# Attention with a depthwise convolution: nine key blocks to a batch, and normalized x kept in DRAM

## The chip, the cores and the metric

The kernel runs on one core of one Trainium2 chip. A time is the device time of one execution in microseconds. Profiled executions carry a record of every instruction of the engines: PE (TensorE), DVE (VectorE), ACT (ScalarE), POOL (GpSimd), and SP (SyncE), which issues nearly all DMAs here.

## The reference

All data is float32. With `ln` a layer norm over the 384 channels of a token, for each of 4 images of 48 x 48 = 2304 tokens:

```
x        (4, 384, 48, 48)                      # 8 heads of 48 channels
local    = batchnorm(depthwise_conv7x7(x))     # 49 taps a channel
q, k, v  = ln(x) @ qkv_w.T + qkv_b
q        = q + ln(local)
out      = softmax(q @ k.T * 48**-0.5) @ v     # per head, 2304 x 2304
y        = x + out @ proj_w.T + proj_b
```

## The kernel before

Channels lie on the 128 partitions in three chunks, two heads side by side (rows 0-47 and 64-111), so that the eight heads make four pairs; the fourth is gathered from the tails of the chunks by DMA (`kt`, `qt`). The tokens of an image fall into six groups of 384 (eight image rows), 24 groups t in all, and into 18 key blocks of 128.

**A group's slots.** The queries of a group t meet all keys of their image, pair by pair, in batches of `BATCH` = 6 key blocks: 3 batches a pair, `NSLOT` = 12 slots a group. In a slot PE first makes the scores of its batch (`scores`, L669, into a ring of three PSUM buffers `r`), ACT turns each into `pt` by an exponential (L673), and then PE weighs the values with the batch of the slot before (`weigh`, L684, into `sums`). Nine `pt` buffers hold the one and a half batches between. Slots 0 to 2 also make the next group's queries (`query_step`, between scores and weighing), slots 5, 8 and 10 the previous group's output projection (`output_step`).

**The end of a pair.** When the last batch of a pair has been weighed, `pair_end` copies `sums` out on ACT, in the middle of the next `scores` (after block `BATCH // 2 - 1`), and sends the softmax denominators to DRAM (`den`). For the last pair of a group, six gathers `ao<-aot` follow. Then `divide` fetches all denominators (`rd`), takes reciprocals on DVE (L601), sends them out (`rden`) and spreads them over the partitions (`rb`); its place is just after the scores of slot 2 of the next group.

**The work beside.** DVE convolves the image for the next group (L242, 147 instructions). `convolve("slot", t, s, half)` emits a number of them twice in each slot; a small plan (`spare`, `share`) fixes how many. Two layer norms run in pieces between: that of the convolved group ("local"), and that of one group of the next image's x (in the groups g = 1 to 5 of the first three images, 15 in all; the sixth group of an image is done while the keys are made). Each piece of a norm goes over several engines: a sum over the chunks and a transpose on DVE, a DMA trip (`parts`, `four`), the centring on DVE (L392), the squares on ACT (L339), the same sum and trip again, a root on ACT (L402 to L404), and the scaling on DVE. For the x of the next image they are spread over slots 3 to 8.

**Order.** For PE, DVE and ACT the order of the program is the order of the engine: each works its instructions one after the other, and one that waits holds up all behind it. SP's order is made by the framework. All six normalized groups of x stay in SBUF (`xn0` to `xn5`). Between two images stands a stage of keys and values (`keys_values`), 216 PE instructions.

Before the first group, a first stage loads the weights, normalizes the first image, makes its keys and values, and convolves its first group (partly on PE, L261).

Of the kernel before, what the change touches and what calls it, by code (L numbers as in the profile page):

```python
# [23 lines left out]
BATCH = 6  # L24
NSLOT = 12
X_SLOTS = 4, 7
OUT_SLOTS = 5, 8, 10
# [15 lines left out]
def unshifted_pass(  # L43
# [56 lines left out]
    xn = {}  # L100

    def load_x(b, g):
        t = big.tile([P, CC, G], F32, tag=f"xn{g}", name=f"xn{b}_{g}")
        load_packed(t, x[b, :, g * G : (g + 1) * G])
        xn[b, g] = t
# [52 lines left out]
    for c in range(CC):  # L158
# [17 lines left out]
        work.tile([P, 2, C], F32, tag="pt", name="pt", bufs=9) for _ in range(PE_TAPS * CC // 6)  # L176
# [6 lines left out]
    load_x(0, 1)  # L183
    load_packed(staged[0], qkv_wT[:, 0:C])
    for g in range(2, NG):
        load_x(0, g)
# [80 lines left out]

    def spare(t, s, half):
        b, g = divmod(t, NG)
        other = 0.0  # L270
        if b + 1 < B and g:
            other += {(3, 1): 2.0, (4, 1): 2.1, (5, 1): 2.0, (8, 0): 2.5}.get((s, half), 0.0)
        if t:
            other += {(2, 0): 0.7, (4, 1): 1.4}.get((s, half), 0.0)
            other += 0.6 if half and s in OUT_SLOTS else 0.0
        if t + 1 < NT:
            first, second = norm_slots(t)
            other += {
                (first - 1, 1): 2.0,
                (first, 1): 2.1,  # L280
                (first + 1, 1): 2.0,
                (second + 1, 0): 4.4,
            }.get((s, half), 0.0)
        return max(0.0, 4.0 - other)

    def norm_slots(t):
        return (6, 9) if t else (8, 10)

    points, room = [], []
    for t in range(NT):  # L290
        if t % NG == 0 and t:
            points += [("kv", t, g, h) for g in range(NG) for h in range(2)]
            room += [4.0, 2.0, 4.0, 2.0, 4.0, 2.0, 4.0, 4.0, 2.0, 4.0, 4.0, 4.0]
        points += [("slot", t, s, h) for s in range(NSLOT) for h in range(2)]
        room += [spare(t, s, h) for s in range(NSLOT) for h in range(2)]
    share = {pt: [] for pt in points}
    at = 0
    for t in range(1, NT):
        due = points.index(("slot", t - 1, norm_slots(t - 1)[0], 0))
        total, n, done, sofar = sum(room[at:due]), CC * KS * KS, 0, 0.0  # L300
        for i in range(at, due):
            sofar += room[i]
            upto = round(n * sofar / total)
            share[points[i]] += [t] * (upto - done)
            done = upto
        at = due
# [9 lines left out]
    def chunk_sum(src):  # L316
        s = work.tile([P, G], F32, tag="sum", name="sum")
        nc.vector.tensor_add(s, src[:, 0, :], src[:, 1, :])  # L318
        nc.vector.tensor_add(s, s, src[:, 2, :])  # L319
        return s  # L320

    def spread_mean(s):

        m = bank()
        nc.tensor.matmul(m[:, :G], lhsT=mean_w, rhs=s, start=True, stop=True)  # L325
        return m

    def spread_sum(src):

        m = bank()  # L330
        project(m[:, :G], lambda c: mean_w, lambda c: src[:, c, :])
        return m

    def centre(src, m):
        nc.vector.tensor_sub(src, src, over_chunks(m[:, :G]))  # L335

    def squares(src):
        sq = work.tile([P, CC, G], F32, tag="sq", name="sq", bufs=1)
        nc.scalar.activation(sq, src, AF.Square)  # L339
        return sq  # L340

    def inverse_root(m):

        y = work.tile([P, G], F32, tag="y", name="y", bufs=1)
        u = work.tile([P, G], F32, tag="u", name="u", bufs=1)
        nc.scalar.activation(u, m[:, :G], AF.Ln, bias=eps)
        nc.scalar.activation(y, u, AF.Exp, scale=-0.5)
        nc.scalar.activation(u, y, AF.Square)
        return m, y, u
# [4 lines left out]
    few = G // 32  # L354

    def sum_out(src):

        s = chunk_sum(src)
        blocks = work.tile([P, G], F32, tag="u", name="blocks", bufs=1)
        part = work.tile([P, few], F32, tag="part", name="part")  # L360
        parts = dram.tile([32, 4, few], F32, tag="parts", name="parts")
        four = work.tile([P, 4 * few], F32, tag="four", name="four")
        nc.vector.transpose(blocks, s)
        nc.vector.tensor_reduce(
            part, blocks.rearrange("p (k i) -> p k i", i=32), AX.X, ALU.add
        )
        nc.sync.dma_start(out=parts.rearrange("i q k -> q i k"), in_=part)
        nc.sync.dma_start(
            out=four,
            in_=parts.rearrange("i q k -> i (q k)")  # L370
            .rearrange("(o i) f -> o i f", o=1)
            .to_broadcast([4, 32, 4 * few]),
        )
        return four

    def sum_in(four):
        s = work.tile([P, few], F32, tag="few", name="few")
        nc.vector.tensor_reduce(
            s, four.rearrange("p (q k) -> p k q", k=few), AX.X, ALU.add
        )  # L380
        return s

    def spread(s):
        y = work.tile([P, G], F32, tag="y", name="y", bufs=1)
        nc.vector.transpose(
            y, s.rearrange("p (k i) -> p k i", i=1).to_broadcast([P, few, 32])
        )
        return y

    def centre_by(src, four):  # L390
        y = spread(sum_in(four))
        nc.vector.scalar_tensor_tensor(src, over_chunks(y), -1.0 / C, src, ALU.mult, ALU.add)  # L392

    def variance(four):
        s = sum_in(four)
        nc.vector.tensor_scalar(s, s, 1.0 / C, LN_EPS, ALU.mult, ALU.add)
        return s

    def few_root(v):
        y = work.tile([P, few], F32, tag="few_y", name="few_y")  # L400
        u = work.tile([P, few], F32, tag="few_u", name="few_u")
        nc.scalar.activation(u, v, AF.Ln)  # L402
        nc.scalar.activation(y, u, AF.Exp, scale=-0.5)
        nc.scalar.activation(u, y, AF.Square)  # L404
        return v, y, u

    def few_newton(v, y, u):
        nc.vector.tensor_mul(u, u, v)
        nc.vector.scalar_tensor_tensor(u, u, -1.0, y, ALU.add, ALU.mult)
        nc.vector.scalar_tensor_tensor(y, u, -0.5, y, ALU.mult, ALU.add)  # L410
        return spread(y)

    def newton(m, y, u):
        nc.vector.scalar_tensor_tensor(u, m[:, :G], eps, u, ALU.add, ALU.mult)
        nc.vector.scalar_tensor_tensor(u, u, -1.0, y, ALU.add, ALU.mult)
        nc.vector.scalar_tensor_tensor(y, u, -0.5, y, ALU.mult, ALU.add)
        return y
# [129 lines left out]
    def query_end(t, rs):  # L547
# [3 lines left out]
        nc.vector.tensor_mul(acc, acc, over_chunks(rs))  # L551
# [105 lines left out]
    def scores(t, s):  # L657
# [4 lines left out]
        for kb in range(k0, k0 + BATCH):  # L662
# [9 lines left out]
            pt = work.tile([P, 2, G], F32, tag="pt", name="pt", bufs=9)  # L672
            nc.scalar.activation(pt, r[:, :, :G], AF.Exp, scale=SCALE)  # L673
            batch.append((kb, pt))
            if kb == k0 + BATCH // 2 - 1:
                pair_end()
        weighing.append((t, p, batch))
# [35 lines left out]
    src = xn[0, 0]  # L713
    m = spread_sum(src)
# [3 lines left out]
    centre(src, m)  # L718
    sq = squares(src)
# [3 lines left out]
    m = spread_sum(sq)  # L723
    root = inverse_root(m)
# [3 lines left out]
    nc.vector.tensor_mul(src, src, over_chunks(newton(*root)))  # L728
# [3 lines left out]
    for g in range(NG):  # L732

        last = g == NG - 1
        src = accs[0] if last else xn[0, g + 1]
        making = keys_values(0, g)
        next(making)
        convolve_first(8 if last else 4)
# [4 lines left out]
        s = chunk_sum(src)  # L743
# [4 lines left out]
        m = spread_mean(s)  # L748
        convolve_first(4)
        centre(src, m)  # L750
        sq = squares(src)
        if not last:
            next(making)
        convolve_first(3)
        m = spread_mean(chunk_sum(sq))
        root = inverse_root(m)
        next(making)
# [6 lines left out]
        if last:  # L764
            r, r2 = ring(), ring()
            for u, m in enumerate((r[:, 0], r[:, 1], r2[:, 0])):
                query_step(0, u, m)
        else:
            first_products(5 if g < 4 else 0)
        convolve_first(8)  # L770
        rs = newton(*root)
        if last:
            query_end(0, rs)
        else:
            nc.vector.tensor_mul(src, src, over_chunks(rs))

    for t in range(NT):
        b, g = divmod(t, NG)
        if g == 0 and b:
# [3 lines left out]
            src = xn[b, NG - 1]  # L783
            for gk in range(NG):
                making = keys_values(b, gk)
                next(making)
                if gk == 4:
                    rs = few_newton(*root)
                    nc.vector.tensor_mul(src, src, over_chunks(rs))
                convolve("kv", t, gk, 0)  # L790
                next(making)
                if gk == 3:
                    root = few_root(variance(four))
                convolve("kv", t, gk, 1)
                if gk == 0:
                    four = sum_out(src)
                if gk == 1:
                    centre_by(src, four)
                if gk == 2:
                    four = sum_out(sq)  # L800
                next(making)
                if gk == 1:
                    sq = squares(src)
        following = t + 1 < NT
        coming = None
        sent = {}
        first, second = norm_slots(t)
        for s in range(NSLOT):
            scores(t, s)

            if s == 2 and t:
                rb = divide(t - 1)
            if s == 0 and not following:

                ending = big.tile([P, CC, G], F32, tag="xn0", name="ending")
                nc.gpsimd.memset(ending[:, 0, :], 0.0)
                for j in range(2):
# [6 lines left out]
                    )  # L824
# [631 lines left out]
```

## Time and profile before

| | |
|---|---|
| median of 3 runs | 3011.69 us (3011.38 to 3012.81) |
| the profiled execution | 3014.8 us, span 3013.0 us, mean granted clock 0.998 |
| PE busy | 2979.3 us (99%), 15698 matmul instructions |
| DVE busy | 2300.9 us (76%) |
| ACT busy | 1560.7 us (52%) |
| DMA | 98.83 MB, 14.3% of the engines' time on the queue of SP |

A row of the instruction groups names the line, the engine, the operation, what it writes and reads, how many there are, their busy time and the mean duration, and how long the engine stood idle before them and for whom. Matmuls overlap in the pipeline, so the mean duration of one (490 ns) is longer than the time between two starts. Each matmul of the program is two instructions in the trace, and those of the two heads of a pair start together (6 to 7 ns apart).

### The profile page before, as it was taken

To read this page: it belongs to the slowest core of one execution; us is meant where nothing else is said; L and a number is where in the kernel's file an instruction comes from. 1 tells how busy PE (TensorE), PEld (TensorE's weight loads), DVE (VectorE), ACT (ScalarE), POOL (GpSimd) and SP (SyncE) were. 2 spreads that over 40 slices of the span, in tenths; PEclk is the share of its full clock that TensorE was granted. 3 is DMA by queue.
4 is the path that set the end of the run, shared out by engine and by line. 5 is a ranking of instruction groups with operands and counts; after the bars stand their busy time and mean duration, and the time that the engine had idled before them with its cause. 6 is when DMAs were issued, how large, how long until landed. Compare 5 with 4: busy or idle time off the path is not lost.

```text
span 3013.0 us, 42331 instructions
## 1 busy us (share of the span) xinstructions
PE 2979.3 (99%) x15698; PEld 1358.1 (45%) x15698; DVE 2300.9 (76%) x4556; ACT 1560.7 (52%) x2385; POOL 24.3 (1%) x71
## 2 busy tenths in 40 slices
PE   7999999999999999999999999999999999999998
PEld 4544444444454444444454444444445444444443
DVE  6899988887666899888755888987876488788411
ACT  4455555555435555555534555555552555555553
POOL 2000000000000000000000000000000000000000
PEclk9999999999999999999999999999999999999999
DMA  6111111011111111111110111012010111100001
GB/s 108 39 25 21 34 36 45 20 38 41 30 26 33 36 33 32 34 35 34 32 30 23 35 38 45 21 34 48 27 30 19 28 27 33 25 26 19 17 26 29
DMA packets 97868, 98.83 MB, mean 33 GB/s; under 512 B 42850, under 2 KB 88435, under 8 KB 97652
## 3 DMA queue, kind: packets, MB, share of 16 engines
q1 hardware_dynamic: 96192, 95.86, 14.3%
q8 instruction: 125, 2.05, 0.3%
q14 instruction: 91, 0.75, 0.1%
q0 software_dynamic: 960, 0.07, 0.0%
q10 hardware_dynamic: 500, 0.11, 0.0%
HBM read 70.19 MB, written 15.24 MB: 28 GB/s over the span
## 4 chain that ended last, share of the span: by engine, by line
PE 95%; DVE 3%; DMA 1%; ACT 0%; issue 0%; POOL 0%; SPq 0%; ACTq 0%; DVEq 0%; POOLq 0%
PE r L669 38%; PE o L684 37%; PE m L422 10%; PE r L422 9%; DVE acc L242 2%; PE o L261 0%; PE m L325 0%; DMA staged<-in_qkv_wT_dram 0%; DMA columns<-bias 0%; PE r L890 0%; DMA bias<-row 0%; DMA taps_in<-in_conv_w_dram 0%; DMA vec<-natural 0%; DVE xn L335 0%; DVE sum L319 0%
## 5 line engine op out<-in xcount | busy, mean ns | idle before, releaser
L673 ACT ACTIVATE pt<-r 128x768 f32<-128x768 f32 x1728 | 1276.3, 812 | 1166.1 <-PE o L684 740.3
L242 DVE SCALAR_TENSOR_TENSOR acc<-slab,vec,acc 128x368 f32<-128x368 f32 (+8 forms) x3429 | 1736.7, 583 | 6.5 <-DMA vec<-natural 3.3
L684 PE MATMUL o<-pt,v 128*49 128x384 f32 x6912 | 1173.8, 489 | 0.1
L669 PE MATMUL r<-q,k 48*128 48x384 f32 x5184 | 908.2, 496 | 0.0
L684 PEld LDWEIGHTS o<-pt,v 128*49 128x49 f32 x6912 | 425.8, 124 | 709.0 <-issue 682.1
L669 PEld LDWEIGHTS r<-q,k 48*128 48x128 f32 x5184 | 439.6, 185 | 467.3 <-ACT pt L673 226.4
L669 PE MATMUL r<-qt,kt 48*128 48x384 f32 x1728 | 300.2, 493 | 0.0
L647 DVE SCALAR_TENSOR_TENSOR xr<-m,pb,xr 128x384 f32<-128x384 f32 x69 | 42.5, 616 | 282.9 <-PE m L422 282.9
L669 PEld LDWEIGHTS r<-qt,kt 48*128 48x128 f32 x1728 | 150.5, 185 | 149.4 <-ACT pt L673 67.8
L422 PE MATMUL r<-xn,w_qk 128*128 128x384 f32 x450 | 152.3, 491 | 0.7 <-ACT q L545 0.7
L422 PE MATMUL m<-ao,w_o 128*128 128x384 f32 x414 | 152.0, 503 | 0.4 <-DVE ao L868 0.4
L422 PE MATMUL m<-xn,w_qk 128*128 128x384 f32 x414 | 152.0, 503 | 0.0
L422 PE MATMUL r<-w_v,xn 128*128 128x384 f32 x432 | 144.5, 487 | 4.2 <-DVE xn L728 2.4
L422 PEld LDWEIGHTS r<-xn,w_qk 128*128 128x128 f32 x450 | 86.7, 193 | 62.4 <-issue 3.0
L318 DVE TENSOR_TENSOR sum<-sq 128x384 f32<-128x384 f32 x47 | 26.1, 555 | 112.7 <-ACT sq L339 112.7
L422 PEld LDWEIGHTS r<-w_v,xn 128*128 128x128 f32 x432 | 81.7, 190 | 62.8 <-issue 4.7
L422 PEld LDWEIGHTS m<-ao,w_o 128*128 128x128 f32 x414 | 73.0, 189 | 74.6 <-issue 13.6
L422 PEld LDWEIGHTS m<-xn,w_qk 128*128 128x128 f32 x414 | 73.0, 189 | 74.2 <-issue 27.8
L462 ACT COPY v<-r 128x384 f32<-128x384 f32 x72 | 32.1, 481 | 134.8 <-PE r L422 134.8
L601 DVE RECIPROCAL rd<-rd 128x24 f32<-128x24 f32 (+2 forms) x25 | 7.5, 301 | 123.6 <-DMA rd<-den 123.6
L458 ACT ACTIVATE k<-r,qkb 128x384 f32<-128x384 f32 x72 | 39.3, 580 | 65.6 <-PE r L422 65.6
L584 ACT COPY ao<-o 49x384 f32<-49x384 f32 x141 | 66.7, 473 | 1.7
(118 smaller groups left out, 821.1 us busy)
## 6 DMA issues: line engine op xcount, KB each, us to landing
xr<-in_x_dram SPq DMA_DIRECT2D x24, 576.0 KB
out_dram<-xr SPq DMA_DIRECT2D x72, 192.0 KB
slab<-in_x_dram SPq DMA_DIRECT2D x32, 378.0 KB
xn<-in_x_dram SPq DMA_DIRECT2D x48, 216.0 KB
rb<-rden SPq DMA_DIRECT2D x48, 216.0 KB
slab<-in_x_dram SPq DMA_DIRECT2D x16, 297.0 KB
slab<-in_x_dram SPq DMA_DIRECT2D x32, 126.0 KB
xn<-in_x_dram SPq DMA_DIRECT2D x48, 72.0 KB
```

What stands on the lines that cost most here:

```text
L242: nc.vector.scalar_tensor_tensor(dst, src, weight, dst, ALU.mult, ALU.add)
L318: nc.vector.tensor_add(s, src[:, 0, :], src[:, 1, :])
L422: nc.tensor.matmul(dst, lhsT=weights(c), rhs=src(c), start=c == 0, stop=c == CC - 1)
L458: nc.scalar.activation(k[:, u, :], r[:, j, :G], AF.Identity, bias=qkb[:, 1, u : u + 1])
L462: nc.scalar.copy(v[:, u + NB, :, 0:HD], r[:, j, :C].rearrange("p (h d) -> p h d", d=HD))
L584: nc.scalar.copy(dst[r : r + HA], sums[r : r + HA, :G])
L601: nc.vector.reciprocal(rd, rd)
L647: nc.vector.scalar_tensor_tensor(xr[:, co, :], m, pb[:, co : co + 1], xr[:, co, :], ALU.add, ALU.add)
L669: nc.tensor.matmul(r[:, j, :G], lhsT=kk[:, blk * P : (blk + 1) * P], rhs=qq, start=True, stop=True)
L673: nc.scalar.activation(pt, r[:, :, :G], AF.Exp, scale=SCALE)
L684: nc.tensor.matmul(sums[r : r + HA, :G], lhsT=values[t // NG, kb // NB][:, kb % NB, 2 * p + j, :], rhs=pt[:, j, :], start=kb == 0, stop=kb ...
```

## The change

- `BATCH` 6 becomes 9 and `NSLOT` 12 becomes 8: two batches a pair. `pt` has 15 buffers in place of 9. `pair_end` is called in `scores` after block 5 of 9 (it was block 2 of 6).
- `xn0` to `xn5` go. A normalized group of x is written to DRAM (`keep_x`) and read back (`fetch_x`) for the keys and for the queries; SBUF holds one raw group (`xa`) and two normalized ones (`xn`).
- The buffers `sum`, `y` and `u` of the norms go; sums, means and roots live in parts of the one buffer `sq` (class `Norm`).
- The pieces of the norms, the output steps (slots 3, 4, 5), the call of `divide` (slot 1) and the plan of the convolution get new places. In the first stage the last part of the last group's keys stands before the second mean, and the convolution's counts there are 13, 4, 3, 7 (8, 4, 3, 8 before).

The core of the diff (the class `Norm` takes over the bodies of the old helpers):

```
-BATCH = 6
-NSLOT = 12
-X_SLOTS = 4, 7
-OUT_SLOTS = 5, 8, 10
+BATCH = 9
+NSLOT = 8
+QUERY_SLOTS = 0, 1, 2
+OUT_SLOTS = 3, 4, 5
...
+    def x_tile(tag):
+        return work.tile([P, CC, G], F32, tag=tag, name=tag, bufs=1 if tag == "xa" else 2)
...
+    def keep_x(b, g):
+        kept[b, g] = dram.tile([P, CC, G], F32, tag=f"kept{g}", name=f"kept{b}_{g}")
+        nc.sync.dma_start(out=kept[b, g], in_=xn[b, g])
+
+    def fetch_x(b, g):
+        xn[b, g] = x_tile("xn")
+        nc.sync.dma_start(out=xn[b, g], in_=kept[b, g])
...
+        time = 6.0
+        if half == 0:
+            time += 2.1 * (s in QUERY_SLOTS) * (t + 1 < NT) + 2.1 * (s in OUT_SLOTS) * (t > 0)
...
+            time -= {(0, 1): 2.2, (1, 1): 4.4, (2, 1): 2.9}.get((s, half), 0.0)
...
+            time -= {(1, 0): 0.7, (2, 0): 1.4}.get((s, half), 0.0)
...
-            pt = work.tile([P, 2, G], F32, tag="pt", name="pt", bufs=9)
+            pt = work.tile([P, 2, G], F32, tag="pt", name="pt", bufs=15)
...
-            if kb == k0 + BATCH // 2 - 1:
+            if kb == k0 + BATCH - 4:
                 pair_end()
+                if between:
+                    between()
...
-        convolve_first(8 if last else 4)
+        convolve_first(13 if last else 4)
...
-        if not last:
-            next(making)
+        next(making)
...
+                if gk < 4:
+                    fetch_x(b, gk + 2 if gk < 3 else 1)
...
+            scores(t, s, between)
+
+            if s == 1 and t:
                 rb = divide(t - 1)
...
+            if s == 2 and t:
+                ao = outputs[t - 1][0]
+                nc.vector.tensor_mul(ao, ao, rb)
+
+            if s == 4:
+                if coming:
+                    load_x(b + 1, g)
+                if g < NG - 1 and t + 2 < NT:
+                    fetch_x(*divmod(t + 2, NG))
+                elif coming and g == NG - 1:
+                    fetch_x(b + 1, 0)
+                    fetch_x(b + 1, 1)
             convolve("slot", t, s, 0)
...
             if weighing[0][0] != t or s:
                 weigh()
...
+            if coming and g:
+                if s == 1:
+                    norm_x.few_centre()
+                    norm_x.squares()
+                if s == 2:
+                    norm_x.few_variance()
+                    norm_x.few_root()
+            if t and following:
+                if s == 5:
+                    norm.few_centre()
+                    norm.squares()
+                if s == 6:
+                    norm.few_variance()
+                    norm.few_root()
             convolve("slot", t, s, 1)
...
+            if coming and g:
+                if s == 0:
+                    norm_x = Norm(xn[b + 1, g - 1])
+                    norm_x.sum()
+                    norm_x.out()
+                if s == 1:
+                    norm_x.sum_squares()
+                    norm_x.out()
+                if s == 2:
+                    norm_x.scale(norm_x.few_newton())
+                    keep_x(b + 1, g - 1)
```

## The prediction

> **What bounds the kernel now.** The page comes first: the span, the busy shares, and the chain that ended last, by engine.
>
> ```profile
> span 3013.0 us, 42331 instructions
> ...
> PE 2979.3 (99%) x15698; PEld 1358.1 (45%) x15698; DVE 2300.9 (76%) x4556; ACT 1560.7 (52%) x2385; POOL 24.3 (1%) x71
> ...
> PE 95%; DVE 3%; DMA 1%; ACT 0%; issue 0%; POOL 0%; SPq 0%; ACTq 0%; DVEq 0%; POOLq 0%
> ```
>
> PE sets the end. The change takes no matmul away, so it can gain only what PE loses between batches, and it loses whatever makes PE wait. Everything then hangs on the order within a slot, so the second view is the timeline, here slot 1 of a group with an x norm, all engines (start, duration, engine, line, what, count):
>
> ```profile
> 591.26 4.21 PE L669 MATMUL r<-q,k 48*128 48x384 f32 x24
> 592.28 2.21 ACT L673 ACTIVATE pt<-r 128x768 f32<-128x768 f32 x3 [1.39 <-PE r L669]
> 594.37 0.97 ACT L584 COPY aot<-o 49x384 f32<-49x384 f32 x2
> 594.87 0.73 SPq L585 DMA_DIRECT2D den<-aot  x2
> 595.40 2.20 PE L422 MATMUL m<-xn,w_qk 128*128 128x384 f32 x6
> 595.65 4.53 SPq L589 DMA_DIRECT2D ao<-aot  x6
> 597.53 4.08 PE L684 MATMUL o<-pt,v 128*49 128x384 f32 x24
> ...
> 600.28 0.53 SPq L598 DMA_DIRECT2D rd<-den  x1
> ...
> 602.14 0.30 DVE L601 RECIPROCAL rd<-rd 128x24 f32<-128x24 f32 x1 [6.62 <-DMA rd<-den]
> ```
>
> PE runs without a gap: scores 4.14 us, query step 2.13, weighing 4.01. The last pair of the previous group is copied out 3.11 us into the slot, and 7.77 us later the denominators are back, where DVE had waited 6.62 us. Over the groups in which DVE waited, copy to reciprocal was 6.8 to 7.9 us, mostly 6.9. Slot 2 had begun at 601.54, so they came back at about its start, which is where `divide` stands.
>
> **Part 1, the batches.** Inside a batch the pairs of matmuls start every 0.3225 us, a key block every 0.645. Twelve make 3.87; so a weighing batch pays 0.14 at its borders, and a scores batch 0.27, of which 0.06 is a wait for the ring (batches without it take 4.08). The ring matters more with nine blocks. Block i needs the exponential of block i - 3 to be over, and ACT is slower than PE, as the first scores of all show:
>
> ```profile
> 145.84 4.15 PE L669 MATMUL r<-q,k 48*128 48x384 f32 x24
> ...
> 146.81 4.32 ACT L673 ACTIVATE pt<-r 128x768 f32<-128x768 f32 x6 [0.28 <-PE r L669]
> ```
>
> Six take 4.32, one alone 0.81, so the step is (4.32 - 0.81) / 5 = 0.70. From block 5 on PE goes at ACT's step: 0.06, and 0.055 more for each of blocks 6 to 8, 0.23 in all. After: scores 18 x 0.3225 + 0.21 + 0.23 = 6.24, weighing 5.80 + 0.14 = 5.94, together 12.18. Before, one and a half slots: 12.21. So 192 slots gain 0.03 each, **-5.5 us**: the ring takes back nearly all that fewer borders give. Bounds: with no ring wait at all 12.18 - 0.23, thus -49; with the slowest three exponentials of the trace (2.35 for three, a step of 0.77), up to +0.07 x 4 blocks x 192 = +54. The step of 0.70 stands in nearly every run of three (2.21), so I keep -5.5.
>
> **Part 2, the x norm behind `divide`.** In the changed order, DVE's queue in slot 1 holds the reciprocal, 13 convolution instructions (14 in group 1; from the plan), the centring of x, 2 more, the sum of squares. ACT's holds six exponentials, the two copies, three exponentials, the query, *the squares of x*, and then the nine exponentials of slot 2. The squares need the centring, so the exponentials of slot 2 wait behind all of this. The pieces, as they are now:
>
> ```profile
> 621.83 0.24 DVE L378 TENSOR_REDUCE few<-four 128x12 f32<-128x48 f32 x1 [0.88 <-DMA four<-parts]
> 622.10 0.58 DVE L385 STREAM_TRANSPOSE y<-few 128x384 f32<-128x384 f32 x1
> 622.71 1.36 DVE L392 SCALAR_TENSOR_TENSOR xn<-y,xn 128x1152 f32<-128x1152 f32 x1
> ...
> 637.42 1.18 ACT L339 ACTIVATE sq<-xn 128x1152 f32<-128x1152 f32 x1
> ```
>
> Let the scores of slot 1 start at 0. The first exponential starts at 1.02 (592.28 - 591.26); the copies follow the sixth, 1.02 + 6 x 0.70 = 5.2 (now 1.02 + 3 x 0.70 = 3.1, as shown). The reciprocal comes 6.9 later, at 12.1. It and the two rows behind it take 0.65 (602.14 to 602.79); 13 convolutions at 0.50 (the row's 1736.7 / 3429 is 0.506, groups at an image's edge 0.47) take 6.5; the centring, 621.83 to 624.07, 2.24: 21.5. The squares end at 22.7.
>
> The scores of slot 2 start at 6.24 + 2.13 + 5.94 = 14.3, and the first exponential is wanted at 15.3. It is 7.4 us late. PE makes three blocks into the ring and stands. Nothing covers this: DVE can't come earlier, since it waits for `rd`, and coming later only makes it worse. Now the same squares stand behind the exponentials of a slot and the centring is long done (622.71 against 637.42).
>
> A stall has a second price. Two gaps of the first stage, first the rows in which PE waited, then the windows after them (columns: length, PE busy, granted clock, DMA share, GB/s):
>
> ```profile
> 31.51 4.11 PE L422 MATMUL r<-w_v,xn 128*128 128x384 f32 x12 [2.42 <-DVE xn L728]
> ...
> 132.72 1.60 PE L325 MATMUL m<-sum,mean_w 128*128 128x384 f32 x2 [4.16 <-DVE sum L319]
> ```
>
> ```profile
> 132.70:136.10 3.40, 3.38 (x6) 0.51 0.02 5
> ...
> 31.50:34.80 3.30, 3.29 (x10) 1.00 0.99 166
> ```
>
> After 2.4 us of idling PE goes on at full clock; after 4.2 us it has half the clock for 3.3 us, with pairs 0.64 apart. A stall of 7.4 lies beyond both. Then blocks 3 to 8 take 4.93 us from the first restart to the start of block 8 (five pairs at half speed, then full), where ACT's step alone would ask 5 x 0.70 = 3.50: 1.43 more. So 8.9 us a group, in 15 groups: **+133 us**. Bounds: without the clock's part 112; with copy to reciprocal 7.9 instead of 6.9, 148.
>
> The Trainium skill (TensorE: Matmul & The Clock Gate, Part 1) says that the clock halves after an idle window of about 3.4 us and comes back after as long a busy one, and that the window runs free of the program. It speaks against this change in the same way; by it alone a stall would cost up to 1.7 us more, an estimate, and the sum would end some 4 us higher.
>
> **Part 3, the rest of a group.** After the stall, DVE has some 13 us of idling at `rd` in a group (now 3 to 7), but its group holds 98 us of work (97.6 to 100.3 busy in 110.4 us in the windows by group) and now lasts 119. Followed on from 21.5: the variance of x is ready at 33, before slot 3 begins at 37.5, so its root on ACT holds nobody. In slot 5 the centring of the local norm ends about when the slot's exponentials do, 3 us before the next are wanted; slot 6 has as much. No stall; the groups without an x norm have the wait for `rd`, but no squares behind it.
>
> **Part 4, x in DRAM.** 24 writes and some 40 reads of 576 KB on SP's queue. Of the reads only those for the keys have a user soon: a group's keys take 69.86 / 6 = 11.6 us, the read waits for its buffer and two gathers and has about 9.5 us left. In the tail now, `rb`, queued behind a 576 KB load, had landed 7.1 us after that load's issue (2982.91 to 2989.96). So 0. If a read took 15 us, 9 of them would each cost 5.5 and a cold start of 1.6: +64. The norm's single buffer adds no wait, since its pieces already follow one another: 0.
>
> **Part 5, the ends.** In the first stage the wait of 4.16 us before 132.72 is filled with the last keys, and its slow clock goes; the five convolutions moved ahead add 0.5 to the norm behind it. The first scores start near 140.5 instead of 145.84: **-5.3** (bounds -6 and 0). At the end, denominators of the first three pairs are copied out 5.2 us into the last slot; copy to end of the scaling by `rb` is 14.2 now (2977.11 to 2991.32); PE is through after 18.1: **+1.3**.
>
> **The sum.** From the profiled execution's 3014.8: - 5.5 + 133 - 5.3 + 1.3 = 3138.3. It stands 3.1 above the median of the runs, so 3135.
>
> **Rivals.** (a) *The squares hold nobody, and the time falls.* If the chain of part 2 ended by 15.3 instead of 22.7, only parts 1 and 5 would be left: 3002, or 2959 with no ring wait. For it: PE never waits now, DVE's pieces lie far from their users. Against it: 12.1 of the chain comes from rows of this trace, before any DVE work. It decides at 15.3 us. Chance 0.08. (b) *The reads of x come late at the three image borders*, in addition: 3135 + 64 = 3199. For it: they stand on SP behind gathers that wait for ACT. Chance 0.07. (c) The forecast's mechanism without the slow clock, 3114, or with a slower denominators' trip, 3150, is within it. Forecast: 0.85.
>
> The range goes from 3080 (stall with warm clock, half of the ring's bound) to 3170 (slow trip and part of the late reads). A measurement here can tell 0.2%, 6 us, from no change. Case (a) gives faster 0.08; same 0.02 for a chain shorter than read; slower 0.90.
>
> **What would show it.** After: the idle time of the x squares on ACT, for DVE, about 9 us in each of 15 groups; DVE's waits for `rd` near 12 us; PE's scores of slot 2 with a gap of 7 us after three blocks and a granted clock near 0.5 behind it; slots of 12.2 us without query or output step. Wrong if groups with and without an x norm take the same time, or if PE stands in the key stages.

## The result, and the profile after

| | before | after |
|---|---|---|
| median of the runs | 3012.25 us (4 runs) | 3148.53 us (4 runs, 3146.11 to 3149.11) |
| the profiled execution | 3014.8, span 3013.0 | 3148.69, span 3146.9 |
| mean granted clock | 0.998 | 0.976 |

The ratio is 1.0451, with an interval of 1.0433 to 1.0469: the change costs 136 us. The page of the changed kernel, in the lines that were shown of before:

```profile
span 3146.9 us, 42287 instructions
...
PE 3011.5 (96%) x15698; PEld 1369.5 (44%) x15698; DVE 2304.6 (73%) x4556; ACT 1543.9 (49%) x2385; POOL 25.2 (1%) x71
...
PE 87%; DVE 5%; ACT 2%; SPq 2%; DMA 2%; issue 2%; ACTq 0%; POOL 0%; DVEq 0%; POOLq 0%
```

PE has the same 15698 instructions, but the chain that ended last now leaves PE for 13% of the span (5% before). PE is busy for 32 us longer with the same work (a slow clock shows as busy time), and the other 102 us of the span are idle time. The waits say where. Their columns are engine, line, what it waited for and from whom, then the total, how often, and the longest.

```profile
DVE rd L623 <- DMA rd<-den: 295.4, 21, 35.7
...
ACT sq L347 <- DVE xa L415: 144.5, 15, 10.3
...
PE r L692 <- ACT pt L696: 105.7, 15, 7.7
```

Read from top to bottom this is the chain: the denominators hold DVE, DVE holds the squares of x on ACT, ACT holds PE's ring, and the last two do so 15 times, once for each group with an x norm. One of the 15 in the timeline, slots 1 and 2 (weight loads left out):

```profile
1156.23 6.31 PE L692 MATMUL r<-q,k 48*128 48x384 f32 x36
...
1161.41 0.99 ACT L606 COPY aot<-o 49x384 f32<-49x384 f32 x2
...
1168.29 0.30 DVE L623 RECIPROCAL rd<-rd 128x24 f32<-128x24 f32 x1 [12.40 <-DMA rd<-den]
...
1168.95 6.83 DVE L252 SCALAR_TENSOR_TENSOR acc<-slab,vec,acc 128x376 f32<-128x376 f32 x13
...
1170.55 2.21 PE L692 MATMUL r<-q,k 48*128 48x384 f32 x12
...
1176.57 1.36 DVE L415 SCALAR_TENSOR_TENSOR xa<-sq,xa 128x1152 f32<-128x1152 f32 x1
...
1177.96 1.16 ACT L347 ACTIVATE sq<-xa 128x1152 f32<-128x1152 f32 x1 [9.71 <-DVE xa L415]
1179.03 2.19 ACT L696 ACTIVATE pt<-r 128x768 f32<-128x768 f32 x3
...
1179.88 6.56 PE L692 MATMUL r<-q,k 48*128 48x384 f32 x24 [7.12 <-ACT pt L696]
```

With slot 1 at 0, the copies start at 5.18, the reciprocal at 12.06, the centring ends at 21.70, the squares end at 22.89. PE makes three blocks (the x12 row) and stands for 7.12 us. The first exponential of slot 2 was due 1.02 after the scores began, at 1171.57, and came at 1179.03: 7.46 late. The granted clock around this gap (length, busy time of PE, PEld, DVE, ACT and POOL, granted clock, DMA share, GB/s):

```profile
1171.00:1174.50 3.50, 1.76 (x12) 0.76 (x8) 3.50 (x8) 0.00 (x0) 0.00 (x0) 1.00 0.67 169
1174.60:1184.70 10.10, 4.82 (x16) 2.73 (x18) 9.72 (x17) 5.39 (x7) 0.00 (x0) 0.50 0.01 1
1184.90:1188.30 3.40, 3.40 (x16) 1.63 (x12) 3.40 (x8) 0.10 (x1) 0.00 (x0) 1.00 0.04 7
```

Half the clock from 1174.6 to 1184.8, so for 4.9 us after the restart. Slot 2 lasts 14.32 us in the groups without an x norm, and 23.3 to 24.9 us in the 15 with one: 143.2 us too long in all, 9.5 each.

### The profile page after: what moved, and what is told of

It reads as the page before. It is cut to its first block, busy times and chain, and to the rows that moved or that the text cites. A ratio compares the mean times of both kernels' runs of the same rounds, so it can differ in the third digit from the quotient of the medians.

```text
span 3146.9 us, 42287 instructions
## 1 busy us (share of the span) xinstructions
PE 3011.5 (96%) x15698; PEld 1369.5 (44%) x15698; DVE 2304.6 (73%) x4556; ACT 1543.9 (49%) x2385; POOL 25.2 (1%) x71
## 4 chain that ended last, share of the span: by engine, by line
PE 87%; DVE 5%; ACT 2%; SPq 2%; DMA 2%; issue 2%; ACTq 0%; POOL 0%; DVEq 0%; POOLq 0%
PE r L692 36%; PE o L709 33%; PE m L444 8%; PE r L444 8%; DVE acc L252 3%; SPq L611 2%; ACT pt L696 2%; DMA rd<-den 1%; DVE xa L415 1%; ACT aot L606 0%; PE o L271 0%; PE m L362 0%; DVE sq L414 0%; DMA staged<-in_qkv_wT_dram 0%; PE r L952 0%
## 5 line engine op out<-in xcount | busy, mean ns | idle before, releaser
L696 ACT ACTIVATE pt<-r 128x768 f32<-128x768 f32 x1728 | 1260.5, 821 | 1161.4 <-PE r L692 593.4
L709 PE MATMUL o<-pt,v 128*49 128x384 f32 x6912 | 1155.3, 489 | 0.0
L692 PE MATMUL r<-q,k 48*128 48x384 f32 x5184 | 943.8, 516 | 105.7 <-ACT pt L696 105.7
L692 PEld LDWEIGHTS r<-q,k 48*128 48x128 f32 x5184 | 450.4, 192 | 598.0 <-ACT pt L696 401.4
L444 PE MATMUL r<-xn,w_qk 128*128 128x384 f32 x360 | 120.3, 486 | 0.7 <-ACT q L567 0.7
L444 PE MATMUL r<-w_v,xn 128*128 128x384 f32 x342 | 114.3, 487 | 1.6 <-DVE xn L439 1.6
L347 ACT ACTIVATE sq<-xa 128x1152 f32<-128x1152 f32 x20 | 23.3, 1163 | 151.3 <-DVE xa L415 144.5
L444 PEld LDWEIGHTS r<-xn,w_qk 128*128 128x128 f32 x360 | 68.3, 190 | 48.7 <-ACT q L567 1.3
L444 PEld LDWEIGHTS r<-w_v,xn 128*128 128x128 f32 x342 | 64.6, 190 | 48.1 <-DVE xn L439 2.2
L350 DVE TENSOR_TENSOR sq<-sq 128x384 f32<-128x384 f32 x47 | 26.2, 557 | 68.4 <-ACT sq L347 68.3
```

The source lines that it names most:

```text
L347: nc.scalar.activation(self.buf, self.src, AF.Square)
L350: nc.vector.tensor_add(self.buf[:, 0, :], src[:, 0, :], src[:, 1, :])
L444: nc.tensor.matmul(dst, lhsT=weights(c), rhs=src(c), start=c == 0, stop=c == CC - 1)
L692: nc.tensor.matmul(r[:, j, :G], lhsT=kk[:, blk * P : (blk + 1) * P], rhs=qq, start=True, stop=True)
L709: nc.tensor.matmul(sums[r : r + HA, :G], lhsT=values[t // NG, kb // NB][:, kb % NB, 2 * p + j, :], rhs=pt[:, j, :], start=kb == 0, stop=kb ...
```

## The experiments

The theory: `divide` in slot 1 puts the denominators' trip ahead of the convolution and the centring on DVE, and the squares of x, which need the centring, stand on ACT ahead of the nine exponentials of slot 2. The rivals: the larger batches themselves (ACT's step and PE's ring), the reads of x, or a cold clock with little idling behind it.

**1. The division one slot later**, everything else as in the change:

```diff
-            if s == 1 and t:
+            if s == 2 and t:
                 rb = divide(t - 1)
...
-            if s == 2 and t:
+            if s == 3 and t:
                 ao = outputs[t - 1][0]
                 nc.vector.tensor_mul(ao, ao, rb)
```

> The call of divide stands after the scores of slot 2 again, and the scaling by rb at the start of slot 3; nothing else differs from the changed kernel. Theory (the x squares wait behind the reciprocal): the denominators are back 12 us into slot 1, before DVE reaches the reciprocal in slot 2, so the centring no longer waits for them; the fifteen slots 2 of 23.3 to 24.9 us become 14.3 us, which takes away 143 us: 3005 us, a few us under the kernel before. Rival (DVE has too little room, with 98 us of work in a group of 110): the stall only moves to a later piece of the norms, and the time stays above 3100 us.

Measured: 3004.65 us (2999.83 to 3010.64, 8 runs) against 3013.36 of the kernel before (12 runs), a ratio of 0.9972 [0.9962, 0.9983]. Slot 2 of such a group in the timeline:

```profile
1106.88 1.18 ACT L347 ACTIVATE sq<-xa 128x1152 f32<-128x1152 f32 x1
...
1109.32 6.32 PE L692 MATMUL r<-q,k 48*128 48x384 f32 x36
1110.34 4.33 ACT L696 ACTIVATE pt<-r 128x768 f32<-128x768 f32 x6 [2.27 <-PE r L692]
...
1110.37 0.29 DVE L623 RECIPROCAL rd<-rd 128x24 f32<-128x24 f32 x1
```

The squares are over before slot 2 begins, its 36 score matmuls run through, and the reciprocal has no wait in front of it. Slot 2 takes 14.32 us in each of these 15 groups, and the waits no longer have a row of PE for the exponentials. So this place of one call is the whole loss of the change, and without it the change beats the kernel before by 0.28%. (The scaling by `rb` moves with the call; experiment 2 leaves both where the change has them.)

**2. The centring ahead of the convolution**, with `divide` left in slot 1. Only DVE's order in slot 1 changes:

```diff
+            if coming and g and s == 1:
+                norm_x.few_centre()
             convolve("slot", t, s, 0)
...
                 if s == 1:
-                    norm_x.few_centre()
                     norm_x.squares()
```

> divide stays in slot 1, but the centring of x stands ahead of the 13 convolution instructions of slot 1's first half, not behind them. Theory (the stall is the excess of one chain): 12.06 to the reciprocal, 0.66, 2.2 for the centring, 1.16 for the squares end at 16.1 us, where the exponential is wanted at 15.3: 0.8 us late, too short for the slow clock, so slot 2 is 15.1 us and 15 x 8.8 = 132 us go: 3017 us. Rival (the slow clock comes with any stall there): 0.8 + 2.2 = 3.0 us remain a group: 3050 us. Rival (the 13 convolutions are not in the chain): no change, 3148 us.

Measured: 3069.76 us (3068.94 to 3074.28, 4 runs), a ratio of 1.0192 [1.0176, 1.0207]: 53 us over the expectation. Slot 2 did what was expected (15.2 us too long in all, down from 143.2). But slot 3 became 49.0 us too long, where it had none of that in the changed kernel. The timeline of slots 2 and 3 in one of the groups:

```profile
1143.64 4.42 PE L692 MATMUL r<-q,k 48*128 48x384 f32 x24 [0.35 <-ACT pt L696]
...
1159.49 0.21 ACT L426 ACTIVATE few_u<-few 128x12 f32<-128x12 f32 x1 [5.73 <-DVE few L421]
...
1160.94 4.42 PE L692 MATMUL r<-q,k 48*128 48x384 f32 x24 [2.67 <-ACT pt L696]
```

In slot 2 PE now stands for 0.35 us (in one group for 1.75, and there it lost its clock as well). In slot 3 the root of the same norm (L426) stands on ACT ahead of the exponentials and waits 5.73 us for the variance, which DVE brings after all its convolutions. In the changed kernel this second wait was hidden: PE had just lost 9.5 us, which gave DVE the time. The expectation had left it out. Some of the 49 us is the clock once more: with the same wait of 2.66 to 2.67 us slot 3 took 17.3 us in three groups where the clock stayed whole, and 18.7 to 20.1 in three where it fell to half.

**3. The same with the root and the scaling in slot 3 instead of slot 2**, on top of experiment 2:

```diff
-                if s == 2:
+                if s == 3:
                     norm_x.few_variance()
                     norm_x.few_root()
...
-                if s == 2:
+                if s == 3:
                     norm_x.scale(norm_x.few_newton())
                     keep_x(b + 1, g - 1)
```

> The kernel of e2, with the variance, the root and the scaling of the x norm in slot 3, not slot 2. In e2 the stall of slot 2 fell to 0.7 to 1.2 us a group (15 us in all) and 49 us stood in slot 3, where ACT's root waited for DVE's variance. Theory (what is left in e2 is that second wait on the same late chain): with the root a slot later DVE has 12 us more, slot 3 is 14.3 us again, and about 49 us go: 3020 us. Rival (slot 3 is long in e2 for want of DVE time): the wait moves to slot 4, and the time stays near 3070 us.

Measured: 3032.59 us (3031.12 to 3036.48, 4 runs), a ratio of 1.0064 [1.0047, 1.0081]. The 49 us of slot 3 are gone (14.32 us again). It is 12 us above the expectation. Slot 2 keeps 19.0 us, 3.2 and 3.3 of them in two groups. The miss is slot 6, which gets 12 us too long in all: about 1.07 in six groups (13.29 instead of 12.22) and 5.5 in another, where the clock fell too. There the squares of the local norm wait on ACT for their centring: with DVE that late, this norm begins to run late as well.

**4. Warm matmuls in the gap.** The changed kernel, with ten matmuls into a bank that nobody reads, placed where PE stands:

```diff
+            if kb == k0 + 2 and s == 2 and b + 1 < B and t % NG:
+                m = bank()
+                for _ in range(10):
+                    nc.tensor.matmul(m[:, :G], lhsT=w_o[:, 0, 0:P], rhs=w_v[:, 0, :], start=True, stop=True)
```

> The changed kernel with ten matmuls of 128 x 384, into a bank that nobody reads, after the third block of slot 2 in the fifteen groups: 6.5 us of work in a gap of 6.4 to 7.7 us. Theory (about 2.2 us of each stall are the half clock after it): PE does not stand, the clock stays whole, blocks 3 to 8 go at ACT's step: 15 x 2.2 = 33 us less, 3115 us. Rival (the clock costs nothing, since ACT sets the pace after the gap as well): 3148 us; or more, if the ten matmuls come in the way.

Measured: 3114.6 us (3110.6 to 3118.85, 4 runs), a ratio of 1.0332 [1.0316, 1.0348]; granted clock 0.998. The scores behind the gap:

```profile
1165.54 4.42 PE L692 MATMUL r<-q,k 48*128 48x384 f32 x24 [0.92 <-ACT pt L696]
```

They take 4.42 us, ACT's pace (4.33 to 4.42 in 14 of the 15 groups); in the changed kernel they take 6.2 to 6.9, on average 6.61. The difference of 2.19, 15 times, is 33 us, and the times differ by 34. The two profiled executions differ by less, 30 us, of which slot 2 makes 29 (143.2 against 114.1): in one group of this one PE still stood for 2.06 us behind the ten matmuls and had half the clock, and the scores took 5.89. Adding 300 instructions made the kernel faster, and the other 110 us stayed: lateness and clock are two separate prices.

**5. A small step on ACT in each slot**, on top of experiment 1, to see whether ACT's step sets the pace of a nine-block batch:

```diff
+    idle = const.tile([P, 12], F32, tag="idle", name="idle")
...
             nc.scalar.activation(pt, r[:, :, :G], AF.Exp, scale=SCALE)
+            if kb == k0 + 1:
+                nc.scalar.activation(idle, ident[:, 0:12], AF.Square)
```

> The kernel of e1 with one small activation (128 x 12, a step of about 0.24 us like the roots of the norms) more behind the second exponential of every slot, 192 in all. Theory (from block 5 on, PE goes at ACT's step, with no slack): each passes to PE one for one, 192 x 0.24 = 46 us over e1, near 3050 us, and a slot without projections goes from 12.2 to 12.4 us. Rival (ACT, busy for 49%, has room): no change to e1.

Measured: 3020.35 us in a single run, 16 more than the median of experiment 1, where 46 were expected. The runs of experiment 1 lie up to 11 us apart, so the slots say more than this one time. The timeline shows why:

```profile
2629.74 0.21 ACT L699 ACTIVATE idle<-ident 128x12 f32<-128x12 f32 x1
...
2629.84 2.92 ACT L697 ACTIVATE pt<-r 128x768 f32<-128x768 f32 x4
```

The insert holds ACT for 0.10 us, not the 0.24 that I had taken from the roots, which wait for one another. Slots went from 12.13 to 12.22 and from 14.26 to 14.35 throughout, and 192 x 0.09 is 17. So the theory holds and the size of the insert was wrong: what ACT takes longer, PE waits for one for one, though ACT is busy for half of the span only.

**6. The last keys back in their old place**, on top of experiment 1:

```diff
-        next(making)
+        if not last:
+            next(making)
         convolve_first(3)
         norm.sum_squares()
         norm.mean()
         norm.root()
-        next(making, None)
+        next(making)
```

> The kernel of e1, with the last third of the first image's last keys back behind the second mean (the convolution's counts stay 13, 4, 3, 7). Theory (the move fills the wait ahead of that mean and saves its slow clock): a wait of some 4 us and half the clock for 3 us come back, the first scores start about 6 us later, near 145 us, and the time is 5 to 6 us over e1: 3010 us. Rival (the norm's chain sets the start, whatever PE does): no change to e1.

Measured: 3011.93 us (3009.45 to 3014.55, 10 runs) against 3013.06 before (16 runs), a ratio of 0.9995 [0.9985, 1.0005]. The second mean of the first stage, without and with the move (the second row is experiment 1's):

```profile
130.79 1.62 PE L362 MATMUL m<-sq,mean_w 128*128 128x384 f32 x2 [4.16 <-DVE sq L351]
```

```profile
130.72 0.88 PE L362 MATMUL m<-sq,mean_w 128*128 128x384 f32 x2 [0.29 <-DVE sq L351]
```

With the keys moved, PE's wait of 4.16 us and the slow mean (1.62 instead of 0.88) go, and the first scores start at 138.27 instead of 144.56. So 6.3 us of the gain of experiment 1, in the two profiled executions, are this move, and the nine-block batches with all the rest come to nothing that can be told from 0. In this kernel the shorter slots (4.8 us, below) are partly given back: in the first group the weighing behind the `vbp` matmuls takes 7.71 us instead of 6.01, and in the last group PE waits 1.42 us for the scaling, which stands a slot later.

**7. Each read of x issued twice**, on top of experiment 1:

```diff
-        nc.sync.dma_start(out=xn[b, g], in_=kept[b, g])
+        for _ in range(2):
+            nc.sync.dma_start(out=xn[b, g], in_=kept[b, g])
```

> The kernel of e1, with every read of a normalized group from DRAM done twice, one after the other, into the same buffer: 39 reads of 576 KB more, and each has its data about twice as late. Theory (the reads are covered): a read takes 3 to 4 us and stands 11 us ahead of its user in the key stages, so PE waits for none: within 3 us of e1. Rival (the reads are near their users, or their traffic slows the denominators' trip): over 15 us more than e1, with PE standing in the key stages.

Measured: 3004.31 us (3000.79 to 3007.27, 7 runs), a ratio of 0.9972 [0.9961, 0.9984]: the same as experiment 1, and the last slots before the key stages, which hold these stages, take 87.79 us in both. Twice the reads cost nothing that shows, so the reads as they are cost nothing that shows.

## Why the prediction was right, point by point

The forecast was 3135 us, in a range of 3080 to 3170; the measured median is 3148.53. Of the 13.5 us between them, 10.4 are a difference in the sum (+123.5 forecast, +133.9 measured in the profiled executions), and nearly all of that is one term, the clock. The other 3 were taken off because the profiled execution of before stood that far above the median of its runs; that of after stands only 0.2 above its own.

**Part 2, the lateness: right in each link.** Forecast and measured, from the start of slot 1: copies 5.2 and 5.18, reciprocal 12.1 and 12.06, end of the centring 21.5 and 21.70, squares over at 22.7 and 22.89, lateness 7.4 and 7.46. That this chain is the cause is shown by experiment 1, which takes the reciprocal out of its head, and by experiment 2, which takes the convolution out of its middle: the stall of slot 2 goes in both.

**Part 2, the clock: the term that was mis-sized.** The forecast was 1.43 us a stall; it is 2.2 (experiment 4). The step that failed is "half the clock for 3.3 us", taken from one gap of the first stage. Behind the 15 gaps the half clock lasted 4.2 to 5.7 us after the restart, 5.0 on average, and in each case it began and ended on one grid of 3.413 us that runs through the whole execution: 3.413 x 3 = 10.24 us in ten gaps, 3.413 x 2 = 6.83 in five. A restart in the middle of such a window has to pay its rest and the next window whole. In the one gap that I had read, the half clock began at 132.75 and ended at 136.16, and PE had restarted at 132.72: nothing was left to pay but the one window. The difference, 15 x (2.19 - 1.43) = 11, is about what the term came out too small by (133 against 143.2). (The 4.93 of the forecast comes out as ten pairs at 0.3225 and half of 3.41; the five slow pairs that it names would make 4.81.)

The other gap was read for more than it shows. "After 2.4 us of idling PE goes on at full clock" held by its place on the grid. In the changed kernel the same twelve matmuls, behind the same wait, ran at half the clock (4.11 us before):

```profile
31.28 5.70 PE L444 MATMUL r<-w_v,xa 128*128 128x384 f32 x12 [2.42 <-DVE xa L439]
```

Before, the 2.42 us lay across an edge of the grid, 1.25 in one window and 1.17 in the next. Here 2.23 of them lay in one window, and the half clock began at its end, at 31.09. The 15 gaps part in the same way: where PE stood for 1.60 us or more of the window in which it stopped, the half clock began with the next window (ten gaps); where it stood for 1.58 or less of it, one window later (five gaps). Over all nine traces the border is less sharp (1.35 to 1.98 us went both ways), but from 27 us on no window with 2.0 us or more of standing was followed by a full clock. So that the forecast's stall of 7.4 us would lose the clock was right, but its two gaps did not show why.

The Trainium skill (TensorE: Matmul & The Clock Gate, Part 1) gives this window as 3413 ns and calls it free-running; the edges in this trace agree (from 1055.09 to 1174.56 there are 35 windows of 3.413). That the clock halves only after an idle window of about 3.4 us, as the prediction takes from there, this trace does not bear out: in ten of the 15 gaps half the clock began 1.6 to 3.2 us after PE had stopped. The "some 4 us higher" of the prediction does not follow from its own "up to 1.7 us more": a restart anywhere in the window would cost 0.85 more on average, which makes some 13 us in 15 stalls, an estimate from the page's window, where 11 were measured. I had weighed the rule and kept the sum at the single row. Read together, the row gives the speed (0.50) and the page's window gives how long: the rest of a window and one more, by estimate 3.4 to 6.8 us.

**Part 1: right.** Slots without a projection take 12.13 to 12.22 with few exceptions (forecast 12.18), and experiment 5 shows that what ACT takes longer passes to PE one for one. That the ring gives back just the difference of the two steps (0.70 against 0.645) fits these times, but no run changes the batch alone. Over the span this part brought some 4.8 us (5.5 forecast), 0.2 for each group.

**Part 3: right, with a condition that I had not seen.** The roots held nobody, as forecast: in the group shown above the variance was ready 33.0 us after the start of slot 1 (33 forecast), and slot 3 began at 38.2 (37.5 forecast). But the margin (33 against 37.5) existed because the stall had moved slot 3 back; experiment 2 took the stall away and met the root 5.7 us late.

**Part 4: right** (experiment 7). A read of 576 KB issued at 859.88 had landed some 3 us later, and its user began at 871.30.

**Part 5: the start right, the end right only in size, and by luck.** First scores at 139.66 (140.5 forecast), a gain of 6.2 (experiment 6: 6.3). At the end the wait for `rb` did not come: the scaling was over at 3127.0, before PE's last weighing at 3128.7. The span after that weighing is still 18.2 us instead of 16.7; the last DVE instruction stands 9.2 us after it in both kernels, so the 1.5 us lie in the last output write or behind it. What makes them wasn't tried.

**Not forecast:** slot 3 of the first group takes 15.92 us. Its weighing runs at half the clock for one window of 3.4 us, after 18 matmul instructions of one column (`vbp`) during which PE shows as busy. In experiment 1 the clock stays full there and the slot takes 14.29. In the other six experiments the slot takes 15.92 to 16.02. Its place on the grid may decide: in the seven executions that lost the clock, 1.7 to 2.2 us of these instructions lay in one window and the clock fell at its end, and in experiment 1 no more than 1.2. But in the kernel before it was 1.7 in one window, and the clock stayed; what parts these cases wasn't tried.

The sum, against the profiled execution of before: 143.2 (slot 2) - 6.2 (start) - 4.8 (slots) + 1.6 (slot 3 of the first group) + 1.5 (end) - 1.4 (the rest, not taken apart) = 133.9 = 3146.9 - 3013.0.

**The rivals.** (a), no late squares, decided at 15.3 us; the chain ended at 22.9. Its price of 3002 was nearly that of experiment 1, 3004.65. (b), late reads, is refuted by experiment 7. The version that beats both kernels is experiment 1.

## What to carry to other kernels

When pieces move between slots, take each instruction that waits on another engine, work out the earliest moment its input can exist from the rows of the trace, and then look at what is queued behind it on its own engine: a division that is itself off the path cost 143 us through two queues. Before trusting a margin behind a stall, ask whether the stall made it; taking the stall away can bring the next one up. Before making batches larger, compare the step of the engine that consumes them with that of the engine that fills them: here 0.70 against 0.645, and nine blocks in place of six won some 5 us of 3013.

## What the runs showed of the hardware that was not expected

- All 15 slow stretches of the granted clock behind the gaps begin and end on one grid of 3.413 us. A gap of 7 us cost 2.2 us through the clock, and ten matmuls in it won this back in 14 of the 15.
- Not the length of a gap alone decides whether the clock falls, but how much of it lies in one window of this grid: the same wait of 2.42 us cost nothing in the kernel before (1.25 and 1.17 in two windows) and one window at half the clock in the changed one (2.23 in one).
- A PE that is busy in the profile can still lose its clock: 18 matmul instructions of one column, 2.3 us, were followed by a window at 0.50 in the changed kernel and in six of the experiments, and by full clock in experiment 1 and in the kernel before.
- A 128x12 activation lasts 0.21 us, but holds ACT for 0.10 where the next instruction doesn't need its result, and for 0.24 to 0.27 in the chain of roots, where it does.
